# Guessing an attention threshold from part of the keys, and starting two blocks of each step inside the stage in front

## The chip, the cores and the metric

The kernel runs on one core of a Trainium2 chip. The metric is the device time of one execution in microseconds (us), the median of several. A core has TensorE (PE), VectorE (DVE), ScalarE (ACT), GpSimd (POOL) and SyncE (SP, which only issues transfers here); each works through its own list of instructions in order, and they wait for one another by semaphores.

## The reference

Four graph layers over x (4096 nodes, 256 features) with a sparse 4096 x 4096 adjacency. The change touches layer 0 alone, the first of them:

```python
h = relu(layernorm(x))
Xf = Xa = h
for n in range(2):
    q, k = Xa @ W1.T @ W2.T, Xa @ W3.T            # 64 wide
    probs = softmax(q @ k.T)                       # 4096 x 4096
    # keep of each row its largest entries, until their sum reaches 0.9
    A = probs * (sorted_cumsum_before < 0.9);  A = A / A.sum(row)
    Xf, Xa = R @ Xf, A @ Xa                        # R: normalised adj + I
    Z = Z + Xf @ U1[n].T + Xa @ U2[n].T
x = x + layernorm(h + Z)
```

Layers 1 to 3 (a graph convolution, graph attention with four heads, a convolution) follow in the kernel and are not touched.

## The kernel before

**The attention step.** A block is 128 query rows; a step works through 32 of them. For a block, PE makes the logits in four quarters of 1024 keys (`logits`, L1151) into PSUM tiles `pl`, of which there are two; ACT turns each into exponentials of the logit less a guess, with their sum (`exponentials`, L1165). No row is sorted: a threshold is searched. ACT counts and sums what exceeds it (`evaluate`, L1184, a sign pass `s` and a relu pass `r`), twice over 1024 of the keys (`s0 r0`, `s1 r1`) and then over all 4096 (`s2 r2`, `s3`), and after each round DVE works out the next threshold (`aim`, L1196, and `update`, a dozen instructions on 128x1 tiles, ending in `next_pair`, L1265). DVE then lists the largest entries below an upper bound (`below` L1373, `segments` L1381, `listing`), decides the exact threshold, and sets the rest of the row to zero (`cut`, L1433). PE sums over the partitions how many entries tie with the threshold (`ties_pe`, L1456), ACT copies the number (`tied`), and DVE branches on it (`drop`, L1441). Then PE transposes the block in eight tiles (`flip`, L1502), ACT copies each (`take`, L1508), and PE multiplies with the values (`attend`, L1517). In step 0 PE also makes the next step's keys and queries of the block from the result (`next_keys`, L1578 for `kt1`, L1580 for `q`, which is stored to DRAM).

A row whose threshold was not found by its list is counted at the end, and a count other than zero makes the program run `general_layers`, which does all layers again in another way.

**The guess.** What is subtracted in the exponential is the same kind of number for every row: mean and variance of its logits, from the first and second moments of the keys. `by_node` (L969) transposes four 128-column pieces of the keys (eight blocks' worth) and ACT copies them to `kn`; `add_moments` (L975) adds their outer product in PSUM; four rounds cover the 32 blocks. `guess` scales the sums (L982 to L988), multiplies them with 512 queries at a time (L997, L998), sums over the features (L1003), and takes 16 small DVE steps (L1016 to L1030, ending in `minus_guess`), once for the first four blocks and once for the other 28.

**The marks.** In step 0, DVE reduces the adjacency, in 128 pieces of 512 KB, to marks of where it has entries (`marking`, L751), one piece at a time, with four pieces loaded ahead by SP. From the marks, `listed_columns` works out each row's list of columns, by 20 rounds of MAX8 and MATCH_REPLACE8 (L803, L804) and a tail; step 1 gathers rows by these lists on POOL (L844).

**The order.** On DVE, ACT and PE the order is written out by hand (`manual_schedule`), POOL and SP are ordered by the scheduler. `front` is a loop over the 32 blocks with a lag of six (layernorm, relu, transposes L1088, copies L1090, keys and queries L963, L1096, L1097), with a piece of marks at every second turn. Afterwards one table of words per step (`ORDERS`) is walked once per period: a word is an operation, `@k` the offset of the block it is applied to, so a period works on about five blocks at different stages. The place `fill` takes further pieces of guess, marks or lists, by a count per period. `period(b)` runs from -3 to 34. In step 0 `close` runs the last three periods, with the moments of the new keys in the period of b = 32, the rest after it, and the guess for step 1 and `verify` behind the last period.

## Time and profile before

| | us |
|---|---|
| median of three executions | 2958.97 (2954.32 to 2965.91) |
| profiled execution | 2964.31 |
| its span, first to last instruction | 2962.5 |
| PE, DVE, ACT, POOL busy in it | 2470.8, 2349.4, 1989.4, 1216.1 |
| front, to its last copy of queries | 0 to about 96 |
| first exponential of step 0, of step 1 | 113.82, 1125.31 |
| first copy of a transposed attention tile (`at`) of step 0, of step 1 | 220.25, 1223.96 |

The profile is one execution by the hardware's profiler. A row of the waits reads: engine, output tile and line that waited, `<-` what it waited for by engine, tile and line; then the sum, the number and the longest of the waits in us. "DVEq L1441" is DVE's branch. In the table of slices each column is a fortieth of the span. `PEclk` is the clock that TensorE was granted, in tenths. Step 0 runs at a steady 25.5 us a block in its middle, step 1 at about 30.6. The last four blocks of step 0 begin their transposes at 990.5, 1018.06, 1045.48 and 1075.45 us.

### The profile page before, as it was taken

The page shows a single profiled execution, that of the slowest core. Times are in us where ns is not written, and L with a number is a line of the kernel's source. Part 1 is how long each engine was busy: PE and PEld are TensorE (multiplying, and loading weights), DVE is VectorE, ACT ScalarE, POOL GpSimd, SP SyncE. Part 2 cuts the span into 40 slices and gives each one's busy share as a digit, 9 for nine tenths or more (in the row PEclk, how much of TensorE's full clock was granted, in tenths as well). Part 3 has the DMA queues.
Part 4 walks back from the last instruction along what each step waited for, and adds up shares of the span by engine and source line. Part 5 has one row for each costly group of instructions (what it writes and reads, how often), then busy time and mean ns, then how long its engine had stood idle before and what let it go on. Part 6 is the DMA issues. An engine that isn't in the chain of part 4 may idle for free. (4 is left out here: it accounts for less than half of the span.)

```text
span 2962.5 us, 44002 instructions
## 1 busy us (share of the span) xinstructions
PE 2470.8 (83%) x12404; PEld 1867.5 (63%) x12404; DVE 2349.4 (79%) x9531; ACT 1989.4 (67%) x3309; POOL 1216.1 (41%) x1246
## 2 busy tenths in 40 slices
PE   6719999999999985599899889999995766898666
PEld 5407777777777762377667666777773545788444
DVE  5689999999999866888878869999965776898000
ACT  3459999999999724887777768888721226898000
POOL 4100000000000000688888865554534775774676
PEclk8859999999999997799999999999997998999788
DMA  7551222222220012244444443443436764553675
GB/s 236 182 186 52 84 81 72 91 81 72 91 67 26 23 47 84 65 131 125 125 120 133 118 120 114 122 129 106 132 102 215 234 190 140 149 159 92 203 219 160
DMA packets 219611, 361.16 MB, mean 122 GB/s; under 512 B 34519, under 2 KB 151772, under 8 KB 219356
## 3 DMA queue, kind: packets, MB, share of 16 engines
q1 hardware_dynamic: 173708, 237.68, 24.9%
q0 software_dynamic: 44672, 120.34, 14.9%
q8 instruction: 101, 1.65, 0.2%
q14 instruction: 154, 1.26, 0.1%
q10 hardware_dynamic: 976, 0.23, 0.0%
HBM read 290.78 MB, written 67.33 MB: 121 GB/s over the span
## 5 line engine op out<-in xcount | busy, mean ns | idle before, releaser
L1184 ACT ACTIVATE unread<-e,next_pair 128x4096 uint8<-128x4096 f32 (+1 forms) x320 | 859.7, 2686 | 188.2 <-DVE next_pair L1265 145.5
L1517 PE MATMUL pa<-va,at 128*128 128x256 f32 x2048 | 502.7, 391 | 4.7 <-DVE t L1639 4.7
L1517 PE MATMUL pa<-h,at 128*128 128x256 f32 x2048 | 468.6, 379 | 0.1
L1517 PEld LDWEIGHTS pa<-va,at 128*128 128x128 f32 x2048 | 381.9, 196 | 71.8 <-issue 21.2
L1151 PE MATMUL pl<-kt,qb 64*128 64x512 f32 x1024 | 285.9, 666 | 150.4 <-ACT e L1165 150.3
L1517 PEld LDWEIGHTS pa<-h,at 128*128 128x128 f32 x2048 | 376.6, 190 | 44.9 <-ACT at L1508 0.3
L1381 DVE MAX8 best<-near 128x8 f32<-128x256 f32 x1024 | 394.7, 415 | 0.1
L1508 ACT COPY at<-pat 128x512 f32<-128x512 f32 x512 | 284.2, 577 | 161.3 <-PE pat L1502 161.1
L844 POOL DMA_INDIRECT vg<-v_d,column x320 | 305.0, 953 | 122.5 <-issue 92.6
L1502 PE MATMUL pat<-ident,e 128*128 128x128 f32 x2048 | 305.0, 280 | 49.0 <-DVEq L1441 24.3
L1502 PEld LDWEIGHTS pat<-ident,e 128*128 128x128 f32 x2048 | 248.3, 144 | 126.2 <-DVEq L1441 42.5
L859 PE MATMUL acc<-vg,ac 128*128 128x256 f32 x768 | 233.6, 448 | 96.4 <-DMA vg<-v_d,column 71.3
L1165 ACT ACTIVATE e<-pl,minus_guess 128x1024 f32<-128x1024 f32 x256 | 284.0, 1122 | 39.0 <-DVE minus_guess L1030 24.6
L1383 POOL COPY eighth<-best 128x16 f32<-128x16 f32 x64 | 13.2, 205 | 695.6 <-DVE best L1381 695.6
L1373 DVE SCALAR_TENSOR_TENSOR near<-e,end_hi 128x4096 f32<-128x4096 f32 x64 | 286.6, 4478 | 0.1
L1433 DVE SCALAR_TENSOR_TENSOR e<-e,end_t 128x4096 f32<-128x4096 f32 x64 | 286.2, 4472 | 0.0
L844 POOL DMA_INDIRECT vg<-far_d,column x160 | 228.6, 1429 | 129.7 <-DVE e L830 81.3
L859 PEld LDWEIGHTS acc<-vg,ac 128*128 128x128 f32 x768 | 157.0, 221 | 168.2 <-DMA vg<-v_d,column 111.6
L1151 PEld LDWEIGHTS pl<-kt,qb 64*128 64x128 f32 x1024 | 91.3, 196 | 259.9 <-ACT e L1165 223.1
L844 POOL DMA_INDIRECT vg<-mixed_d,column x160 | 205.1, 1282 | 67.7 <-issue 44.1
L2184 PE MATMUL acc<-u,tabg 128*65 128x128 f32 x1536 | 194.2, 281 | 42.7 <-DVE u L2169 41.7
L844 POOL DMA_INDIRECT ac<-in_adjt,adj_row x160 | 199.0, 1244 | 54.3 <-issue 42.2
(557 smaller groups left out, 4306.4 us busy)
## 6 DMA issues: line engine op xcount, KB each, us to landing
adj<-in_adjt SPq DMA_DIRECT2D x128, 512.0 KB
ac<-adjc_d SPq DMA_DIRECT2D x64, 384.0 KB
adjc_d<-ac SPq DMA_DIRECT2D x32, 384.0 KB
ac<-adjc_d SPq DMA_DIRECT2D x32, 320.0 KB
vg<-v_d SPq DMA_DIRECT2D x64, 128.0 KB
targets<-steep_d SPq DMA_DIRECT2D x32, 256.0 KB
vg<-v_d,column POOLq DMA_INDIRECT x320
table_d<-tab SPq DMA_DIRECT2D x32, 132.0 KB
```

Of the source, the lines that this page charges most:

```text
L844: nc.gpsimd.indirect_dma_start(out, None, rows, bass.IndirectOffsetOnAxis(ap=index, axis=0))
L859: nc.tensor.matmul(acc, ac[:, k, :], v[:, k, :], start=(k == 0), stop=(k == CHUNKS))
L1151: nc.tensor.matmul(pl[:, r, :], s["qb"][rows], kt[rows, j * 512 : (j + 1) * 512], start=True, stop=True,)
L1165: nc.scalar.activation(s["e"][:, j * 1024 : (j + 1) * 1024], pl.rearrange("p r c -> p (r c)"), AF.Exp, bias=minus_guess[:, b : b + 1], acc ...
L1184: nc.scalar.activation(unread[:, :width], s["e"][:, :width], func, bias=s["at"], scale=-1.0, accum_out=s["signs"] if func == AF.Sign else ...
L1373: nc.vector.scalar_tensor_tensor(near, s["e"], end["hi"][:, b : b + 1], s["e"], op0=ALU.is_lt, op1=ALU.mult, accum_out=s["low"])
L1381: nc.vector.max(best[:, k, :], near[:, k * (N // SEG) : (k + 1) * (N // SEG)])
L1433: nc.vector.scalar_tensor_tensor(s["e"], s["e"], last, s["e"], op0=ALU.is_ge, op1=ALU.mult, accum_out=s["held"])
L1502: nc.tensor.transpose(pt[:, k, :], s["e"][:, c * P : (c + 1) * P], ident)
L1508: nc.scalar.copy(at, s["pt", g])
L1517: nc.tensor.matmul(s["pa"], s["at", g][:, k, :], va[:, c, :D], start=(c == 0), stop=(c == NB - 1))
L2184: nc.tensor.matmul(s["acc"][:, h, :], s["tab"][:, k, h * (DK + 1) : (h + 1) * (DK + 1)], s["u"][:, k, h, :], start=(k == 0), stop=(k == CH ...
```

## The change

In step 0 the guess takes its moments from the first eight blocks of keys, in step 1 from the first 24 (`SAMPLED`). In step 0 three of the four rounds of moments fall away, and the guess's first part is made inside the front, which also makes three of the four quarters of logits and exponentials of blocks 0 and 1 (`EARLY`); from block 16 on, a block's transposes and keys in the front go to a tile of the ring `pmisc` instead of `pl`. Marks in the front come at two of three turns. Period -3 of step 0 goes, and `fills` are spread over -2 and -1.

In the drain of step 0, the three rounds of moments of step 1 stand in period 30, the guess's first part in period 31, and the first three quarters and the first two search rounds of step 1's block 0 at the end of 31 and in 32; likewise block 1 in 32. The lists' first step stands in 31 and 13 pairs of MAX8 and MATCH_REPLACE8 after it are spread over 32 and 33. What was made early is remembered in `done` and not made again. The early search rounds take their goal from three of the four sums (`aim_part`); the full sum follows with the last quarter. The queries of the first four blocks are read back into one more tile (`first`), and the sums of the moments lie in a `pl` tile together with the guess's. In `listed_columns` the tile for the scratch room is laid out anew, which is left out here, as is `enter`, which hands the tiles of a step to it later. The values `va1` of step 1 are loaded after period -3 instead of -1.

```diff
+SAMPLED = (8, 24)
...
-    def add_moments(r, pm):
+    def add_moments(r, pm, last):
         for k in range(4):
             nc.tensor.matmul(
-                pm[:, : P + 1], kn[:, k, :P], kn[:, k, :], start=(r == 0 and k == 0), stop=(r == 3 and k == 3)
-            )
-    def guess(n, pm):
-        nc.vector.tensor_scalar_mul(mk[:DA, :DA], pm[:DA, :DA], 1.0 / N)
-        nc.vector.tensor_scalar_mul(mk[DA:, :DA], pm[DA:, DA:P], 1.0 / N)
+                pm[:, : P + 1], kn[:, k, :P], kn[:, k, :], start=(r == 0 and k == 0), stop=(r == last and k == 3)
+            )
+    def guess(n, pm, psts, first, nodes):
+        nc.vector.tensor_scalar_mul(mk[:DA, :DA], pm[:DA, :DA], 1.0 / nodes)
+        nc.vector.tensor_scalar_mul(mk[DA:, :DA], pm[DA:, DA:P], 1.0 / nodes)
         both = sm.tile([P, 1], F32, name="both")
-        nc.vector.tensor_scalar_mul(both, pm[:, P : P + 1], 1.0 / N)
+        nc.vector.tensor_scalar_mul(both, pm[:, P : P + 1], 1.0 / nodes)
+        yield
         nc.tensor.matmul(pm[:, 256:257], fold, both, start=True, stop=True)
...
+        mean = l0.tile([P, 1], F32, name=f"mean{n}")
         for lo, hi in ((0, 1), (1, 8)):
-            squares = {}
+            squares, pst = {}, psts(lo)
             for g in range(lo, hi + 1):
...
+                    if g == 0:
+                        yield
+                        nc.vector.tensor_copy(mean, pm[:, 256:257])
...
+                if g == 0:
+                    yield
                 if g > lo:
                     for r in range(4):
...
-                    if lo:
-                        yield
+                    yield
...
-    def front(h0, kt, xs, marked):
+    def front(h0, kt, xs, marked, early):
...
-            if i >= 10 and i % 2 == 0:
+            if i >= 8 and i % 3 != 2:
                 some(marked, 1)
             if 0 <= o + 1 < NB:
                 relu(o + 1)
             if 0 <= o < NB:
-                if o % 2 == 0:
-                    pls[o // 2] = ps.tile([P, 2, 512], F32, name="pl")
-                pt = pls[o // 2][:, o % 2, :256].rearrange("p (k i) -> p k i", k=DC)
+                if o >= 2 * SAMPLED[0]:
+                    pls[o] = ps.tile([P, 512], F32, name="pt", tag="pmisc")
+                elif o % 2 == 0:
+                    both_ = ps.tile([P, 2, 512], F32, name="pl")
+                    pls[o], pls[o + 1] = both_[:, 0], both_[:, 1]
...
-            if 0 <= o - 2 < NB and (o - 2) % 8 == 7:
+            if 0 <= o - 2 < SAMPLED[0] and (o - 2) % 8 == 7:
                 by_node(kt, (o - 2) // 8)
-            if 0 <= o - 3 < NB and (o - 3) % 8 == 7:
-                add_moments((o - 3) // 8, pm)
-        guesses = guess(0, pm)
-        next(guesses)
+            if 0 <= o - 3 < SAMPLED[0] and (o - 3) % 8 == 7:
+                add_moments((o - 3) // 8, pm, SAMPLED[0] // 8 - 1)
+            if o - 4 == SAMPLED[0] - 1:
+                pst = ps1.tile([P, NB, 2], F32, name="pst", tag="pa")
+                guesses = guess(0, pm, lambda lo: pst, near[:, :512], SAMPLED[0] * P)
+            if o - 4 >= SAMPLED[0] - 1:
+                early(o - 3 - SAMPLED[0], guesses)
         return guesses
+    EARLY_GUESSES = (1, 1, 1, 1, 1)
+    EARLY = {
+        6: [(0, "logits0")],
+        7: [(0, "exps0")],
+        9: [(1, "logits0")],
+        10: [(1, "exps0")],
+        14: [(0, "logits2")],
+        15: [(0, "exps2")],
+        17: [(1, "logits2")],
+        18: [(1, "exps2")],
+    }
...
-        def logits(b, half):
+        def logits(b, js):
             s = state[b]
-            if half == 0:
+            if js[0] == 0:
                 s["sums"] = small("sums", 4)
                 s["qb"] = wk.tile([P, P], F32, name="qb")
                 nc.sync.dma_start(s["qb"], q_d[n][:, b * P : (b + 1) * P])
+                s["made"] = set()
             s["pl"] = []
-            for j in (2 * half, 2 * half + 1):
+            for j in js:
+                if j in s["made"]:
+                    continue
+                s["made"].add(j)
                 pl = ps.tile([P, 2, 512], F32, name="pl")
...
+        def aim_part(b):
+            goal, skip = small("part_goal"), small("skip", 4)
+            state[b]["part_goal"] = goal
+            nc.vector.scalar_tensor_tensor(
+                skip[:, :3],
+                state[b]["sums"][:, :3],
+                (1.0 - TOP_P) / 3.0,
+                fours[:, :3],
+                op0=ALU.mult,
+                op1=ALU.mult,
+                accum_out=goal,
+            )
+            yield
         def measured(b, k):
             s = state[b]
-            width, goal = (PART, end["goal"][:, b : b + 1]) if k < 2 else (N, s["full_goal"])
+            width, goal = (PART, s.get("part_goal", end["goal"][:, b : b + 1])) if k < 2 else (N, s["full_goal"])
...
+                if "part_goal" in s:
+                    yield from aim(b)
...
-            calls[f"logits{h}"] = of_block(logits, h)
+            calls[f"logits{h}"] = of_block(logits, (2 * h, 2 * h + 1))
             calls[f"exps{h}"] = of_block(exponentials)
+        calls["logits2"], calls["exps2"] = of_block(logits, (2,)), of_block(exponentials)
...
+        done = set()
+        def early(b, *names):
+            for name in names:
+                if name in calls:
+                    done.add((name, b))
+                    calls[name](b)
+                else:
+                    steps, _, *k = chains[name]
+                    for _ in line(steps, b, *k) if k else chain(aim_part(b), update(b, 0)):
+                        pass
+                    lines[(steps, b, *(k or (None,)))] = iter(lengths[steps] * [None])
+        def period(b, fills=(), pieces=((),) * 4, inserts={}):
             pieces = iter(pieces)
@@ -1869,41 +1934,17 @@
                     for fill, k in zip(fills, next(pieces)):
                         some(fill, k)
                 elif name in calls:
-                    calls[name](b + int(off))
+                    if (name, b + int(off)) not in done:
+                        calls[name](b + int(off))
                 else:
                     woven(name)(b + int(off))
-                if name in ("take1", "take3", "take5") and b + int(off) == NB - 1:
-                    some(between, 2)
-        def moments(pm):
-            for r in range(3):
-                by_node(kt1, r)
-                yield
-                add_moments(r, pm)
-                yield
-        def close(lists):
-            for g in range(4):
-                cols = slice(g * 1024, min((g + 1) * 1024, (NB - 2) * P))
-                nc.sync.dma_start(near[:, cols], q_d[1][:, cols])
-            some(lists, 1)
-            pm = ps.tile([P, 2, 512], F32, name="pl").rearrange("p r c -> p (r c)")
-            period(NB, between=moments(pm))
-            period(NB + 1)
-            some(lists, 10)
-            for b in range(NB - 2, NB):
-                nc.scalar.copy(near[:, b * P : (b + 1) * P], state[b]["q"])
-            by_node(kt1, 3)
-            add_moments(3, pm)
-            period(NB + 2)
-            guesses = guess(1, pm)
-            next(guesses)
-            verify()
-            return guesses
-        return period, verify, close
+                for insert in inserts.get(name, ()):
+                    insert()
+        def query(b):
+            return state[b]["q"]
...
+        period, verify, enter, early, query = layer0_step(0, kt0)
+        period1, verify1, enter1, early1, _ = layer0_step(1, kt1)
+        def ahead(i, guesses):
+            some(guesses, EARLY_GUESSES[i] if i < len(EARLY_GUESSES) else 0)
+            for b, words in EARLY.get(i, ()):
+                early(b, *words.split())
         with tc.tile_pool(name="front", bufs=1) as xs, tc.manual_schedule(engines=MANUAL):
-            guesses = front(h0, kt0, xs, marked)
+            guesses = front(h0, kt0, xs, marked, ahead)
         own = st.enter_context(tc.tile_pool(name="own0", bufs=1))
         with tc.manual_schedule(engines=MANUAL):
-            period, verify, close = layer0_step(0, h0, kt0, own, marked)
-            early = {
-                -3: ((0, 2), (0, 2), (3, 2), (0, 2)),
-                -2: ((3, 4), (9, 4), (9, 4), (9, 4)),
-                -1: ((0, 3), (0, 3), (0, 3), (0, 3)),
-            }
-            for b in range(-3, NB):
-                period(b, (guesses, marked), early.get(b, ((0, 0),) * 4))
+            enter(h0, own, marked)
+            fills = {-2: ((2, 3), (2, 3), (2, 3), (2, 3)), -1: ((0, 4), (0, 4), (0, 4), (0, 4))}
+            for b in range(-2, NB - 2):
+                period(b, (guesses, marked), fills.get(b, ((0, 0),) * 4))
             some(marked, NB * QUARTERS)
+            pm = ps.tile([P, 2, 512], F32, name="pl")
+            first = adj_pool.tile([P, CA, P], F32, name="adj").rearrange("p l i -> p (l i)")[:, :512]
+            nc.sync.dma_start(first, q_d[1][:, :512])
             lists = listed_columns(marks, e_pool.tile([P, N], F32, name="e"), ps)
-            guesses = close(lists)
+            def sums_of(lo):
+                if lo:
+                    return ps1.tile([P, NB, 2], F32, name="pst", tag="pa")
+                return pm[:, 1, : 2 * NB].rearrange("p (b k) -> p b k", k=2)
+            guesses = guess(1, pm[:, 0], sums_of, first, SAMPLED[1] * P)
...
+            def ahead1(b, words):
+                return lambda: early1(b, *words.split())
...
+            period(
+                NB - 2,
+                inserts={
+                    "take1": [nodes(0)],
+                    "take2": [sums(0)],
+                    "take3": [nodes(1)],
+                    "take4": [sums(1)],
+                    "take5": [nodes(2)],
+                    "take6": [sums(2)],
+                    "take7": [guessing(1)],
+                },
+            )
+            period(
+                NB - 1,
+                inserts={
+                    "take1": [guessing(1)],
+                    "attend1": [guessing(1)],
+                    "take3": [guessing(1), listing(1)],
+                    "flip4": [guessing(1)],
+                    "attend7": [ahead1(0, "logits0")],
+                    "turn": [ahead1(0, "exps0 logits2 exps2 s0 r0")],
+                },
+            )
+            queries()
+            period(
+                NB,
+                inserts={
+                    "cut": [ahead1(0, "u0")],
+                    "ties": [ahead1(0, "s1 r1")],
+                    "drop": [listing(1), ahead1(0, "u1")],
+                    "take1": [listing(1), ahead1(1, "logits0")],
+                    "take2": [listing(2), ahead1(1, "exps0 logits2 exps2 s0 r0")],
+                    "take3": [listing(1), ahead1(1, "u0 s1 r1")],
+                    "take4": [listing(1), ahead1(1, "u1")],
+                    "take5": [listing(2)],
+                    "take6": [listing(1)],
+                    "take7": [listing(1)],
+                    "turn": [listing(1)],
+                },
+            )
+            period(
+                NB + 1,
+                inserts={
+                    "keys": [last_queries, ahead1(0, "logits1 exps1")],
+                    "xa_pe": [listing(2)],
+                    "copy_xa": [ahead1(0, "s2 r2")],
+                    "h_pe": [verify],
+                },
+            )
+            period(NB + 2)
     with ExitStack() as st:
         s1 = st.enter_context(tc.tile_pool(name="s1", bufs=1))
         vg_pool = st.enter_context(tc.tile_pool(name="vg1", bufs=3))
         va1 = s1.tile([P, NB, D], F32, name="va1")
         with tc.manual_schedule(engines=MANUAL):
-            period, verify, close = layer0_step(1, va1, kt1, s1, vg_pool)
+            enter1(va1, s1, vg_pool)
             fill = by_turns(guesses, lists)
-            pieces = {-3: (0, 3, 2, 3), -2: (2, 3, 2, 2), -1: (2, 2, 99, 0)}
+            pieces = {-3: (3, 3, 2, 3), -2: (2, 3, 2, 2), -1: (2, 2, 99, 0)}
             for b in range(-3, NB + 4):
-                period(b, (fill,), [(k,) for k in pieces.get(b, (0, 0, 0, 0))])
-                if b == -1:
+                period1(b, (fill,), [(k,) for k in pieces.get(b, (0, 0, 0, 0))])
+                if b == -3:
                     for q in range(8):
                         bs = slice(q * NB // 8, (q + 1) * NB // 8)
                         nc.sync.dma_start(va1[:, bs, :], blocks(heads_d)[:, bs, :])
-            verify()
+            verify1()
```

## The prediction

> **What bounds the kernel now.** The order of views was: the page's table of forty slices, then the busy time by stretch, the waits inside the two poor stretches, and the single instructions where the long waits end.
>
> A slice of the span is 74 us; digits are tenths busy.
>
> ```profile
> PE   6719999999999985599899889999995766898666
> ...
> DVE  5689999999999866888878869999965776898000
> ACT  3459999999999724887777768888721226898000
> ...
> PEclk8859999999999997799999999999997998999788
> DMA  7551222222220012244444443443436764553675
> ```
>
> Slices 4 to 13 are step 0 of the attention at its steady pace: all three engines at 9, no DMA limit. Work is lost at the front (slices 1 to 3) and where step 0 drains into step 1 (14 to 16). The change touches nothing of the steady stretches, so its worth is in those two. By stretch (PE, PEld, DVE, ACT, POOL busy us and instructions, granted clock, DMA share, GB/s):
>
> ```profile
> 97.00:220.00 123.00, 44.88 (x164) 22.07 (x163) 93.82 (x297) 66.14 (x78) 0.38 (x2) 0.65 0.53 178
> ...
> 1118.00:1222.00 104.00, 45.43 (x144) 20.62 (x144) 80.99 (x327) 63.85 (x74) 23.35 (x18) 0.63 0.24 71
> ```
>
> The first runs from the end of the front to the first transposed attention tile of step 0, the second likewise for step 1. PE has 45 us of work in each; DVE is nearest to full (76% and 78%). The reader sees a latency chain of DVE and ACT, not a throughput limit. The waits, for 85 to 220, 1000 to 1120 and 1120 to 1240 us:
>
> ```profile
> ACT unread L1184 <- DVE next_pair L1265: 29.2, 4, 16.8
> ACT e L1165 <- DVE minus_guess L1030: 16.6, 1, 16.6
> DVE marks L751 <- DMA adj<-in_adjt: 7.0, 9, 1.8
> ```
>
> ```profile
> DVE mk L982 <- PE pl L975: 16.3, 1, 16.3
> ...
> PE pat L1502 <- DVEq L1441: 7.5, 3, 4.2
> ```
>
> ```profile
> ACT unread L1184 <- DVE next_pair L1265: 20.9, 5, 8.1
> ACT unread L1184 <- DVE steep L1249: 8.5, 3, 4.5
> ...
> ACT e L1165 <- DVE minus_guess L1030: 8.0, 1, 8.0
> ```
>
> ACT cannot start a step's first exponential before DVE has the guess (16.6 and 8.0 us), and then waits for each new threshold behind DVE's marks. Where ACT restarts (start, us, instruction, idle before):
>
> ```profile
> 113.82 1.11 ACT L1165 ACTIVATE e<-pl,minus_guess 128x1024 f32<-128x1024 f32 x1 [16.56 <-DVE minus_guess L1030]
> 161.42 3.71 ACT L1184 ACTIVATE unread<-e,next_pair 128x4096 uint8<-128x4096 f32 x1 [16.84 <-DVE next_pair L1265]
> 194.52 3.71 ACT L1184 ACTIVATE unread<-e,next_pair 128x4096 uint8<-128x4096 f32 x1 [8.84 <-DVE next_pair L1265]
> ```
>
> ```profile
> 1125.31 1.11 ACT L1165 ACTIVATE e<-pl,minus_guess 128x1024 f32<-128x1024 f32 x1 [8.04 <-DVE minus_guess L1030]
> ```
>
> **The change, first place: the front.** Three of four rounds of by_node and add_moments go: 3 x (1.06 + 1.06) = 6.4 us of PE and 3 x 0.58 of ACT. Six quarters of logits come in, four PE records each. Sixteen records took 6.2 us at 115, so 1.56 us a quarter; two took 1.12 us at 97, so 2.24. Six are 9.4 to 13.4 us, and PE gets 3 to 7 us more. Six exponentials of 1.1 us fall on ACT, busy 31.6 of 97 us. DVE gets six more marks of 1.2 us and the guess's first part (two 0.7 us passes, sixteen small ones of 0.19): 8 to 12 us, against 42 idle us of which 31.8 are waits for PE's keys. In the second half a block's pt tile moves from the logits' buffers to the other ring of two, so its transposes wait for the copy two blocks back; the copies already set the pace there (0.4 to 0.5 us a block), so I add nothing. If that ring stalls, it costs up to 0.4 us x 16. Front end: 95.6 to 99, +3.5, ends 0 and +10.
>
> A rule speaks against new PE work here. The Trainium skill (TensorE: Matmul & The Clock Gate, "What's actually happening") says that the array's clock is halved after an idle window of about 3.4 us and is freed only by as much sustained work. A quarter would then be 3.1 us, six 18.7, the front's end about +9 and the whole sum -37 instead of -42. The trace grants 0.84 to 0.86 in the front's middle and 1.0 in its last 17 us, and its slowest quarter there is 2.24; I go by the row, 1.6 to 2.2, and keep the rule for the upper end.
>
> **From the front to the first attend of step 0.** Before, guess and marks hold DVE from 98.95 to 113.8, then four exponentials reach 120.0, where s0 stands. After, blocks 0 and 1 have three quarters ready, one quarter is left: logits 1.6, exp 1.1, so s0 at about 101.4 (-18.6). r2 of block 0 ends at about 117 (136.2 before). Period -3 and eight marks (9.7 us of DVE) leave this stretch; 28 remain, of 36. The s3 of block 0 came 25 us after that, with marks in between; with three or four fewer it comes at about 138 (161.4). The s3 of block 1, 58 us after r2 before, at about 173 (194.5), since there the last 17 marks run into DMA: 0.5 MB each lands in 1.6 to 1.75 us at the 300 to 328 GB/s seen, against 1.2 us of DVE. The two qb loads no longer stand in SP's queue between adj loads (they stopped it 113 to 125 and 164 to 173), so adj is fed without a break. First attend 199.5 against 219.6: -20. Bounds: -8 if the DVE chain between s0 and attend keeps its 100 us and only the guess's 14.9 minus the front's growth is saved; -26 if adj never limits. I take -20, near the DVE sum: 93.8 - 9.7 - 6 = 78 us of work in 100.
>
> **Second place: the drain.** Three rounds of moments (2.1 us PE each, kn copy 0.58) move from the period of block 31's attention to the one two earlier, which is full: +5 us. The next period gets the guess's first part from the sums of 24 blocks and the lists' first step (L986, L997, L1003, L778: 3.5 us of PE) and three logits quarters of step 1's block 0 (4.7): +7 to 8 us on PE. On ACT three exponentials, s0 and r0 (5.7 us) stand ahead of tied for block 31; behind tied wait the branch L1441 and all flips of that block. Against it: the cut of block 31 (1070.77) no longer stands behind the lists' first step, which waited 8.3 us for pt. The flips of block 31 so start at about 1090.5 instead of 1075.45: +15. In the last period -7 of moments and -2.2 of logits leave, three quarters of block 1 (4.6) and about 3 us of stalls come: even. kt of block 31 is copied at about 1125 instead of 1110.06. Bounds for the drain: +5 (PE's 4.2 us wait and ACT, 41 busy of 118, hide the rest) and +30 (everything inserted is serial). Cover of the moved lists (11 pairs of 2.58 us): DVE's idle 16.3 us at 1101.7 to 1118 and the periods' other gaps; without it, +12.
>
> **The restart of step 1.** Before, from kt at 1110.06: guess to 1125.3, four exponentials, three rounds of search, r2 of block 0 done at 1156.3 (+46). After, the guess and two rounds are behind it: keys, logits 1.6, exp 1.1, s2 and r2 3.7 each: done 10 us after kt, 1135, -21. Then DVE's leftovers (7 list pairs 18.1, seven L998 passes of 0.75, found's checks 3.2, small ones) fill 30 us before the update: s3 of block 0 about 1155 (1165). Block 1 has three quarters and two rounds too: its r2 ends at 1166 (1187.9). From there as before; the first attend 1200 against 1222.6: -22, ends -8 and -32. The lists' gathers start at about 1166 (1193 before), so POOL isn't late. qb and first loads are small (64 and 256 KB) in a stretch where DMA is at 0.2 to 0.3: nothing.
>
> **Sum.** -20 - 22 = -42 us: the steps after keep their lengths and shift whole. The profiled execution took 2964.3 us with a span of 2962.5; the median shown is 5.3 below it. 2959 - 42 = 2917. With the bounds -26 - 32 and -8 - 8: 2901 to 2943.
>
> **Rivals.** (1) Half of it: the front saves its 20 but the restart is held by DVE's leftovers (80% of DVE used there) and step 1's gathers, or the other way round: about -20, 2939. For it: the 8.5 us waits on steep show DVE to be the chain of the restart; against it, its work total falls. (2) The drain is serial: +30 instead of +15 makes the second place -7; with the lists' +12 uncovered it is +5, and with the front at its poor end, -8, the sum is -3: 2956, no change. For it: PE is at 104 of 118 us in the drain and its queue is in order; against it: the waits of 4.2 and 16.3 us are room. (3) Slower: the guess from 1024 of 4096 keys (3072 in step 1) is too far off, and a row's threshold falls outside its list. Then found isn't all ones, the last check sends the program into general_layers, which does every layer again: above the 2110 us that the attention takes here, over 5000 in all. One row of 8192 decides it; the guess only sets the scale and the start of a search that goes on for the same number of rounds with the true sums, and in the arithmetic of the kernel's formulas on the given inputs the fullest list holds 28 of 32 and 38 of 40: very unlikely.
>
> **How the numbers follow.** Forecast 0.66, rival 1 0.19, rival 2 0.11, rival 3 0.04. The time is the forecast's, 2917, with its own range 2901 to 2934. 2896 to 2949 takes in the half gain and the better ends and leaves 2 in 10 out, mostly above. 0.5% is 14.8 us, about what a measurement of this kernel tells from none. Faster by more: the forecast and most of rival 1, 0.82; within: the rest of it and most of rival 2, 0.12; slower 0.06.
>
> **What would show it.** ACT's first exponentials before 80 us in the front; s0 of block 0 about 101; s3 at 138; first at copy of step 0 near 200 and of step 1 some 42 us earlier than 1224, near 1182. Periods of step 0 unchanged at 25.5 us. The 16.6 and 8.0 us waits for minus_guess gone, the flips of block 31 15 us later relative to their start of the steady stretch. Wrong if the front ends after 105, if next_pair waits above 30 us remain before the first attend, or if PE waits on ACT's e at several quarters in the drain.

## The result, and the profile after

The changed kernel takes 2944.7 us (median of six, 2943.4 to 2947.1) against 2961.6 for the kernel before beside it (2954.3 to 2965.9): a ratio of 0.9944, interval 0.9931 to 0.9958, 17 us less. Forecast were 42 us less. The profiled execution fell from 2964.3 to 2943.4 us, 21 less, and its trace is laid beside the one of before. The table of slices of the changed kernel:

```profile
PE   5729999999999986798988989999995776898666
...
DVE  5789999999999879888878879999965776898000
ACT  2469999999999835887867878788621226898000
...
PEclk8769999999999987899999999999997998999788
DMA  6651222222220013244444434333437765553675
```

The two weak places are still there: slices 1 to 3 are hardly fuller, while 15 to 17 are (8, 6 and 7 for PE where 8, 5 and 5 stood; the forecast called them 14 to 16). Two stretches say it more sharply, from the front's end to step 0's first attention tile, and the restart of step 1 (columns as before: PE, PEld, DVE, ACT, POOL, clock, DMA share, GB/s):

```profile
106.00:214.00 108.00, 40.30 (x126) 21.99 (x124) 84.62 (x278) 59.27 (x66) 0.38 (x2) 0.60 0.53 176
1116.00:1192.00 76.00, 38.70 (x128) 20.64 (x127) 69.88 (x262) 49.28 (x53) 27.97 (x25) 0.64 0.39 115
```

From the last queries of the front to step 0's first attention copy it was 124.6 us and is 107.8. From the copy of block 31's keys to step 1's first attention copy it was 113.9 us and is 76.1, with DVE busy for 92% of the stretch shown. ACT restarts here in the changed kernel:

```profile
106.81 1.11 ACT L1197 ACTIVATE e<-pl,minus_guess 128x1024 f32<-128x1024 f32 x1 [2.94 <-PE pl L1183]
...
107.92 1.14 ACT L1216 ACTIVATE unread<-e,ones 128x1024 uint8<-128x1024 f32 x1
```
```profile
147.55 3.71 ACT L1216 ACTIVATE unread<-e,next_pair 128x4096 uint8<-128x4096 f32 x1 [4.14 <-DVE next_pair L1312]
```
```profile
187.99 3.71 ACT L1216 ACTIVATE unread<-e,next_pair 128x4096 uint8<-128x4096 f32 x1 [15.91 <-DVE next_pair L1312]
```

The wait for the guess is gone, but the chain starts at 107.9 instead of the 101.4 forecast, and the 15.9 us before the last pass over block 1 (`s3`, forecast at 173, found at 188.0) are a wait that should have shrunk.

How far the changed kernel is ahead of the one before, by the same instruction in both traces (us; minus is earlier):

| | forecast | found |
|---|---|---|
| last queries copied in the front (95.7 before) | +3.5 | +10.3 |
| first attention copy of step 0 (220.3) | -20 | -6.5 |
| the same of block 28 (991.8) | -20 | -5.8 |
| the same of block 31 (1076.3) | -5 | +9.4 |
| first attention copy of step 1 (1224.0) | -42 | -30.0 |
| block 16 of step 1 (1723.5) | -42 | -26.4 |
| block 21 of step 1 (1886.3) | -42 | -26.8 |
| block 24 of step 1 (1979.8) | -42 | -20.6 |
| end of the span (2962.5) | -42 | -20.9 |

The blocks of step 0 keep their length: 27.7 us in the middle in both traces, not the 25.5 given above. A front does not take the same time in every execution. In three traces with the front of before (its own and those of two runs below), step 0's first attention copy came at 220.3, 222.7 and 226.4 us, in four with the changed front at 212.1 to 214.3: the gain there is 6.5 us in this pair and 9.8 between the means.

So there are three questions: why the front and the start of step 0 gave 6.5 instead of 20; whether the drain did what it seems to have done; and what took 9 us back inside step 1.

### The profile page after: what moved, and what is told of

Same layout as the page of the kernel before. It is cut to its first block, busy times and chain, and to the rows that moved or that the text cites. A ratio compares the mean times of both kernels' runs of the same rounds, so it can differ in the third digit from the quotient of the medians.

```text
span 2941.6 us, 43924 instructions
## 1 busy us (share of the span) xinstructions
PE 2463.4 (84%) x12356; PEld 1864.1 (63%) x12356; DVE 2351.0 (80%) x9538; ACT 1986.3 (68%) x3305; POOL 1221.3 (42%) x1246
## 5 line engine op out<-in xcount | busy, mean ns | idle before, releaser
L1183 PE MATMUL pl<-kt,qb 64*128 64x512 f32 x1024 | 278.1, 653 | 115.2 <-ACT e L1197 112.1
L846 POOL DMA_INDIRECT ac<-in_adjt,adj_row x160 | 235.2, 1470 | 56.0 <-issue 41.1
L846 POOL DMA_INDIRECT vg<-mixed_d,column x160 | 205.0, 1281 | 67.0 <-issue 44.4
L846 POOL DMA_INDIRECT vg<-far_d,column x160 | 191.7, 1198 | 85.9 <-issue 48.5
```

The lines of the kernel that those rows point to most:

```text
L846: nc.gpsimd.indirect_dma_start(out, None, rows, bass.IndirectOffsetOnAxis(ap=index, axis=0))
L1183: nc.tensor.matmul(pl[:, r, :], s["qb"][rows], kt[rows, j * 512 : (j + 1) * 512], start=True, stop=True,)
```

## The experiments

The first four runs were made on another chip, where step 1's first half ran at 43 us a block instead of 31 and the kernel before took 3261 us; they are compared with it there, and with each other.

**The front: when the first marks come.** DVE early in the front, before and then changed, with the instruction of ACT that waited in the changed one:

```profile
18.98 0.27 DVE L1054 SCALAR_TENSOR_TENSOR x<-x,x 128x4 f32<-128x4 f32 x1
...
25.14 1.22 DVE L751 TENSOR_REDUCE marks<-adj 128x8 f32<-128x1024 f32 x1 [2.54 <-DMA adj<-in_adjt]
```
```profile
25.80 1.22 DVE L754 TENSOR_REDUCE marks<-adj 128x8 f32<-128x1024 f32 x1 [6.57 <-DMA adj<-in_adjt]
26.93 0.15 DVE L1059 SCALAR_TENSOR_TENSOR x<-x,x 128x4 f32<-128x4 f32 x1
```
```profile
27.12 0.60 ACT L1062 ACTIVATE h<-e,x,x 128x256 f32<-128x256 f32 x1 [10.83 <-DVE x L1059]
```

The first mark now comes one loop turn sooner, ahead of the shift (L1059; L1054 before) that ACT's next four relus need. Its piece of the adjacency lands no sooner than before: the kernel before waited 2.5 us for it, but behind that shift, which it had made at 19.0. The next run makes the first mark at turn 15 of the loop instead of 9. The keys of block 2 came 8.7 us late, and 7.4 were still missing at block 9.

```diff
-            if i >= 8 and i % 3 != 2:
+            if i >= 15 and (i % 3 != 2 or i < 27):
                 some(marked, 1)
```

> The changed kernel with the same 22 marks in the front, but the first one five loop turns later, so that it no longer stands ahead of the third group's shift and relu while its adjacency piece is still in flight. Theory (the front's 10 us are one wait of 6.6 us for the first adjacency piece and what it starts): the front ends near 97.5 instead of 105.9, the first attention copy of step 0 comes near 205 instead of 213.7, and the time falls by about 8 us to 2936. Rival (the front is long because of the logits and marks put into it): the front still ends at 103 or later and the time stays within 3 us of 2944.7.

Measured: 3229.2 us, ratio 0.9899 (0.9878 to 0.9921). Block 2's queries were ready at 23.0 instead of 29.7 us (the run of the front alone, below, has the front of the changed kernel on the same chip), and block 9's at 44.4 instead of 50.4: the wait was what the theory says. But blocks 10 to 31 then took 64.7 us instead of 57.1, and the front ended at 109.1, not 97.5. The first attention copy came at 216.5 against 214.3. So the wait is real, and something took more than its worth back. Two things differ there: the marks stand closer together, one at each of twelve turns, and TensorE's granted clock was 0.84 from 44 to 109 us, against 0.91 from 50 to 107 in the front alone. Which of the two cost the 7.6 us is not shown.

**The start of step 0: marks ahead of a goal.**

```diff
-            fills = {-2: ((2, 3), (2, 3), (2, 3), (2, 3)), -1: ((0, 4), (0, 4), (0, 4), (0, 4))}
+            fills = {-2: ((2, 3), (2, 3), (2, 3), (2, 3)), -1: ((0, 2), (0, 2), (0, 2), (0, 2))}
```

> The changed kernel with two marks instead of four at each fill of period -1, eight fewer ahead of block 2's first goal; the marks' words of the later periods make up for them. Theory (after the front DVE is the limit, and marks stand ahead of the thresholds): the wait of 15.9 us for a threshold before the second pass over block 1 shrinks by 8 to 10 us, the first attention copy of step 0 comes near 205, the time near 2936. Rival (the adjacency loads or the search's own latency set it): the copy stays within 2 us of 213.7.

Measured: 3223.6 us, ratio 0.9881 (0.986 to 0.9901). The first attention copy came at 199.8 instead of 214.3, 14.6 us for eight marks of 1.2 us, since the DMA waits that stood before some of them went too (5.4 us in the front alone, 1.3 here). The restart in question, in this run:

```profile
174.03 3.71 ACT L1216 ACTIVATE unread<-e,next_pair 128x4096 uint8<-128x4096 f32 x1 [0.81 <-DVE next_pair L1312]
```

15.9 us of waiting have become 0.8. The marks put off come back in later periods, where most cost nothing: 1.9 of the 14.6 us are lost again by block 28, in two periods that had no marks and now have three each (28.0 and 27.8 us instead of 27.1 and 26.8).

**The two halves.** In one run the drain is that of before, in the other the front is; the core of each edit:

```diff
-            for b in range(-2, NB - 2):
+            for b in range(-2, NB):
                 period(b, (guesses, marked), fills.get(b, ((0, 0),) * 4))
...
+            period(NB, inserts={k: [lambda: some(two, 2)] for k in ("take1", "take3", "take5")})
+            period(NB + 1)
+            some(lists, 10)
...
+            guesses = guess(1, pm, sums_of, near[:, :512], N)
+            some(guesses, 5)
+            verify()
```

(Here `two` makes three rounds of moments.)

> Only the front's half of the change; the drain of step 0 and the restart of step 1 are those of the kernel before. Theory (the two halves add, and a shift of step 0 passes to the end whole): step 1's first attention copy 6.5 us earlier than before, the time 6 us below before, ratio 0.998. Rival (the front's gain is lost later, in step 1): no difference from before.

```diff
-SAMPLED = (8, 24)
+SAMPLED = (32, 24)
...
-            if i >= 8 and i % 3 != 2:
+            if i >= 10 and i % 2 == 0:
...
+    EARLY_GUESSES = (5,)
+    EARLY = {}
...
+            for b in range(-3, NB - 2):
```

> Only the drain's half of the change; front and first periods of step 0 are those of the kernel before. Theory (the restart gives 24 us at step 1's first attention copy and step 1 takes some 9 back, since its first half is paced by GpSimd's gathers): 1200 us for that copy, the end about 15 us earlier than before, ratio 0.995. Rival (what step 1 took back was an accident of one profile): the end 24 us earlier, 0.992.

Measured: the front alone 3260.7, ratio 0.9995 (0.9982 to 1.0008); the drain alone 3235.9, ratio 0.9909 (0.9883 to 0.9935). By these times the drain carries the whole gain. The traces say where the front's half went. It was 12.1 us ahead of the run with the old front at step 0's first attention copy (214.3 to 226.4) and still 11.5 at block 28; step 0 keeps a lead. Inside step 1, between blocks 21 and 23, it fell behind that run by a further 5.8 us, at the place that block 22 below is about. The 15 us expected of the drain alone became 25: the drain alone does not lose those 6 us, and the rest of the difference is not explained (step 1's first half runs otherwise on this chip).

**Step 1: do the gathers take the lead back?** Between blocks 0 and 16 of step 1 the lead fell from 30.0 to 26.4 us. POOL is busy there for 400 of 505 us, nearly all of it with gathers. The next two runs replace 160 of the 320 gathers of that half.

```diff
-                for i in range(CHUNKS):
-                    gather(ac[:, i, :], adj_rows, adj_row[:, i, d : d + 1])
+                nc.sync.dma_start(ac[:, :CHUNKS, :], adjt[d, :, :CHUNKS, :])
```

The changed kernel itself was run again beside them.

> The changed kernel itself beside the experiments of this call. Theory and rival agree: ratio 0.994 if the chip is like the first; on a chip where step 1's first half is slowed by its gathers the ratio may differ, since more or less of the lead is taken back there.

> The changed kernel, but step 1 fetches the adjacency rows of its first half not by five gathers a block on GpSimd but by one plain load of the same size from the same array; the rows are other ones, so layer 0's mixed values and all that follows are not the reference's. 160 of 640 gathers go. Theory (the gathers of step 1's first half set its pace, 320 of them at 1.65 us each): its periods fall from 31 to about 28 us, 40 us less in all, and the lead of step 1's first attention copy over the kernel without these gathers (next run) is still whole at step 1's end. Rival (the engines' own work sets the pace): under 10 us less.

> The kernel before with the same replacement of the row gathers by plain loads, which again leaves out the right rows. Theory: 40 us less than the kernel before, and 24 to 30 us more than the changed kernel with the same replacement, instead of the 17 between the two whole kernels. Rival: the distance between the two stays 17.

Measured: changed 2944.2 (ratio 0.9936, 0.9914 to 0.9958); without the row gathers 2913.0 for the changed kernel and 2934.9 for the one before. The gathers do pace that half, though by 31 and 28 us, not 40. Without them the lead is 31.6 us at the first attention copy and 31.6 at block 16, where it had fallen by 3.6 with them. It then goes to 29.2 by block 21, where the two whole kernels stood at 26.8. So the gathers account for some 2 to 4 us of what was lost. But the distance of these two kernels is 21.9, not 24 to 30, and the drop between blocks 21 and 24 is there as before (29.2 to 23.2). It had another cause.

**Step 1: block 22.** In the trace of the changed kernel, on DVE behind the cut of that block:

```profile
1884.72 4.48 DVE L1482 SCALAR_TENSOR_TENSOR e<-e,end_t 128x4096 f32<-128x4096 f32 x1
...
1889.72 0.28 DVE L1492 TENSOR_SCALAR drop<-eights,end_extra,end_t 128x8 f32<-128x8 f32 x1
...
1890.12 4.41 DVE L1495 MATCH_REPLACE8 e<-drop,e 128x4096 f32<-128x4096 f32 x1
```

`drop` works only where an entry ties with its row's threshold. The trace of before has no instruction of it; this one has one block with it, and so have the front alone and the two runs with other marks, while the drain alone has none. The guess is subtracted in the exponent, so another guess rounds all entries of step 0, and with them step 1's rows, otherwise. The front alone has the changed guess in step 0 only, the drain alone in step 1 only: the tied block came with step 0's guess, and it takes back some 6 us of what the front's half gives. The next experiment starts from a kernel that takes both findings on the marks together:

```diff
-            if i >= 8 and i % 3 != 2:
+            if i >= 12 and i % 3 != 2:
...
+            fills = {-2: ((2, 4), (2, 4), (2, 4), (2, 4)), -1: ((0, 2), (0, 2), (0, 2), (0, 2))}
```

> The changed kernel with the first mark of the front three turns later (20 marks there, not 22, no denser than before), four instead of three at each fill of period -2 and two instead of four in period -1. Theory (the first mark's wait for its piece costs the front 6 us, and marks ahead of block 2's goal 14 us): the front ends near 100, the first attention copy of step 0 near 195, and the ratio is about 0.008 below that of the changed kernel beside it. Rival (the marks put off come back as a block of work at the end of the marks or the front is slow for its own sake): the ratio stays within 0.003 of it.

Measured: 2928.7, ratio 0.9884 (0.9857 to 0.9911), 15.5 us below the changed kernel beside it where 24 were expected. The front ended at 101.9 (104.3 beside it), the first attention copy of step 0 came at 198.4 (212.1); 195 was expected. This and the three later runs that keep this front show what the first mark's place was worth: they end it at 98.9 to 101.9 us, 100.3 in the mean, where four traces of the changed front have a mean of 105.5 and three of the old one 97.0. With another constant on top:

```diff
-            nc.vector.scalar_tensor_tensor(v, y, -1.2816, v, op0=ALU.mult, op1=ALU.add)
+            nc.vector.scalar_tensor_tensor(v, y, -1.28, v, op0=ALU.mult, op1=ALU.add)
```

> The kernel with later and fewer marks, and in both guesses the factor -1.2816 replaced by -1.28; every row's threshold search starts from slightly other numbers, so that all exponentials are rounded otherwise, and no instruction is added or moved. Theory (in step 1's block 22 one row's entry ties with its threshold only in the rounding that the new guess brings, and the branch then runs a pass of 4.4 us over the block): with other rounding no tied block appears in the trace, step 1's periods are even there, and the time is 6 us below that of the kernel with later and fewer marks. Rival (the 6 us there come from the order or from transfers): the period of block 22 is long again.

Measured: 2922.2, ratio 0.9845 (0.9828 to 0.9861). No instruction of `drop` is in its trace, and its lead over before is 40.8 us at block 21 and 40.9 at block 24, where that of later and fewer marks falls from 38.8 to 32.6. The 6.2 us were the tied block. The order of the work is the same in both runs: that one guess meets a tie and another does not is chance.

**The drain: ScalarE ahead of the tie count.**

```diff
-                    "turn": [ahead1(0, "exps0 logits2 exps2 s0 r0")],
...
-                    "cut": [ahead1(0, "u0")],
-                    "ties": [ahead1(0, "s1 r1")],
-                    "drop": [listing(1), ahead1(0, "u1")],
-                    "take1": [listing(1), ahead1(1, "logits0")],
...
+                    "ties": [ahead1(0, "exps0")],
+                    "drop": [listing(1)],
+                    "take1": [listing(1), ahead1(0, "logits2 exps2 s0 r0")],
+                    "take2": [listing(1), ahead1(0, "u0 s1 r1")],
+                    "take3": [listing(2), ahead1(1, "logits0"), ahead1(0, "u1")],
...
```

> The kernel with later and fewer marks, but in the drain the first exponentials and search passes of step 1's block 0 stand behind the last block's keys and its copy of the tie count on ScalarE, and are spread over the takes. Theory (5.7 us of ScalarE ahead of that copy hold up the last block's branch and transposes): block 31's first attention copy comes 5 to 6 us earlier, step 1's first attention copy about 4 us earlier, and the time is some 4 us below that of later and fewer marks. Rival (the restart is paced by VectorE's lists and checks): block 31 earlier, step 1's first copy unchanged.

Measured: 2922.4, ratio 0.9851 (0.9834 to 0.9867). Both traces on ACT, later and fewer marks first:

```profile
1062.35 0.59 ACT L1587 COPY zt<-pt 128x512 f32<-128x512 f32 x1 [3.79 <-PE pt L1582]
1062.83 1.12 ACT L1197 ACTIVATE e<-pl,minus_guess 128x1024 f32<-128x1024 f32 x1
...
1068.79 0.57 ACT L1607 COPY hu<-pu 128x512 f32<-128x512 f32 x1
...
1072.09 0.14 ACT L1511 CAST tied<-pkq 1x1 int32<-1x1 f32 x1
```

```profile
1057.56 0.59 ACT L1587 COPY zt<-pt 128x512 f32<-128x512 f32 x1 [3.79 <-PE pt L1582]
1058.04 0.59 ACT L1607 COPY hu<-pu 128x512 f32<-128x512 f32 x1
...
1060.45 0.14 ACT L1511 CAST tied<-pkq 1x1 int32<-1x1 f32 x1
```

From `zt` to `tied` 9.7 us became 2.9. Block 31's first copy came 11.9 us earlier, 8.6 of them from the drain (this run was 3.3 us ahead already at step 0's first copy, the front's doing). Step 1's first copy came at 1175.1 instead of 1183.5: 8.4 us earlier, 5.1 more than it brought along, and at step 1's last block 8.4 were left. So the theory held, in the drain and at the restart, and the rival did not. The run with both edits, below, says the same beside the one with the other constant alone: 8.1 us of its own at block 31, 4.8 at step 1's first copy, 4.9 at its last block. Some 3.5 of the 8.6 us do not arrive. DVE is busy for 66.3 of the 73 us from 1102 to 1175 there, so it has little room at the restart; that this is what keeps the 3.5 back is argued, not shown. The 2922.4 and the 2928.7 were measured on two chips, and the intervals of the two ratios overlap.

**The front: what the early quarters cost.**

```diff
-    EARLY = {
-        6: [(0, "logits0")],
-        7: [(0, "exps0")],
...
-    }
+    EARLY = {24: [(0, "logits0 exps0")]}
```

> The changed kernel without the early quarters of the front: only the first half of block 0 is made, after the last keys; block 1 wholly later. Guess and marks in the front stay. Theory (the front's second half is not longer for the six quarters): the front still ends within 1.5 us of 105, and the first attention copy of step 0 comes 4 to 8 us later. Rival (the six quarters lengthen the front by 7 us or more): it ends near 98.

Measured: 2963.4 in its single timed execution, 2967.4 for before. With less to do the front ended 14.3 us later, at 120.3, not at 98 or 105. Both theories were wrong. The same edit again, and a run with products in the places of the quarters that nothing reads:

```diff
+            for j in {6: (0, 1), 9: (0, 1), 14: (2,), 17: (2,)}.get(i, ()):
+                pl = ps.tile([P, 2, 512], F32, name="pl")
+                for r in range(2):
+                    rows = slice(r * DA, (r + 1) * DA)
+                    nc.tensor.matmul(pl[:, r, :], ident[rows], kt0[rows, j * 512 : (j + 1) * 512], start=True, stop=True)
```

> The kernel without early logits once more. Theory (its slow front is TensorE at half clock, because no stretch of the second half keeps TensorE busy long enough): granted clock near 0.5 from 80 us to the front's end, which comes near 119 again. Rival (an accident of one execution): clock above 0.8 and the front's end near 104.

> The kernel without early logits, and at the places where the changed kernel makes the six quarters, as many products of the same shape into the same buffers, which nothing reads. Theory (the products lift the clock, and the clock sets the front's pace): granted clock near 1.0 from 80 us on and the front's end at 102 to 106, though TensorE has more to do. Rival (the pace has another cause): the front's end near 119 as without them, or later.

Measured: 2959.2 and 2951.5 (2962.9 for before). The stretch from 80 to 104 us of the changed kernel, of the repeat, and of the unread products (PE busy and instructions first, clock third from the end):

```profile
80.00:104.00 24.00, 18.01 (x125) 13.49 (x122) 17.02 (x41) 12.85 (x28) 10.85 (x14) 1.00 0.72 225
```
```profile
80.00:104.00 24.00, 17.67 (x76) 15.54 (x76) 13.04 (x36) 6.59 (x16) 9.37 (x12) 0.50 0.54 179
```
```profile
80.00:104.00 24.00, 17.90 (x114) 13.14 (x111) 15.66 (x40) 8.19 (x19) 11.04 (x15) 0.93 0.69 214
```

The front ended at 120.7 in the repeat and at 107.7 with the unread products. TensorE is busy 18 of 24 us in all three; at half clock it gets 76 instructions done, at full clock 114 to 125. Four key products took 1.06 us in the slow front and 0.61 in the fast one. Products that nothing reads give the front 13.0 us back, and with them the clock: it is the clock that sets the pace here, not the work that the quarters add. The kernel before, with its rounds of moments in that half, was granted 0.86 from 60 to 80 us and 1.00 from 80 to 97.

**Together.** The run with the tie count first, with the other constant:

> Later and fewer marks, the tie count's copy first, and the other guess constant, together. Theory (the three causes are independent): no tied block, the time 6 us below that of the kernel with the tie count's copy first, 2916, ratio 0.983. Rival: the ratio stays at 0.985.

Measured: 2918.5 us (2918.1 to 2918.8), ratio 0.9849 (0.983 to 0.9868), 25.7 us under the changed kernel's 2944.2. No tied block in the trace, and the lead of 46 us is the same at blocks 16 and 31 of step 1 (46.4 and 46.2). Beside the run without the other constant (2922.4, on another chip) that is 4 us, and the ratio stays at 0.985, as the rival has it; the intervals overlap. The 6 us are seen in the traces alone: from block 21 to 24 the run without the other constant takes 100.2 us, this one 93.4.

## Why the prediction was wrong

Of the 42 us forecast, 13.5 are missing at step 0's first attention copy and 9 were lost inside step 1; the restart gave 2 more than forecast.

*The front, +3.5 forecast, +10.3 found, outside its bounds by a little.* The forecast's own sign of being wrong, a front that ends after 105, was there (105.9). The step that failed counted DVE's added work against its idle time. The idle time was there, but the first added instruction stood in front of a needed one and waited 6.6 us for a transfer that could not be earlier. With that mark behind the shift, and two marks fewer in the front, the front was 3.3 us longer than the old one between the means, about the +3.5. The logits, weighed at 9 to 13 us, cost no time, and a quarter took 1.0 to 1.1 us of PE. Their price was misread: the two records of 1.12 us at 97 are a whole quarter (in the changed kernel four records take the same 1.13), and the 1.56 of 115 was measured at a clock of 0.50 to 0.76, so doubling it to 3.1 halved the clock twice. The rule of the Trainium skill on the clock (TensorE: Matmul & The Clock Gate, "What's actually happening") was put forward as speaking against the added products, at 3.1 us each. The traces show its other side, that work frees the clock: with the products it was 0.93 to 1.00 from 80 to 104 us, without them 0.50, and the front is then 14 us longer.

*From the front to the first attention, 100.5 us forecast, 107.8 found.* The sum of DVE's work was about right (84.6 us found, 78 forecast); that the chain would shrink with it was not. 28 marks were counted by their total and not by where they stand: the 16 of period -1 stood ahead of the threshold that block 1's last pass waits for, and eight fewer gave 14.6 us.

*The drain and the restart, +15 and -37 forecast, +15.1 and -39.4 found.* Right in size, and the moved work did leave the restart. `tied_first` shows the ScalarE term: ACT's inserted work delays block 31 by 8.6 us, and 5.1 of them reach step 1's first copy. That DVE's leftovers set the pace of the rest, as the forecast's step for s3 had it, fits its 92% there and was not tested.

*"The steps after keep their lengths and shift whole."* Held in step 0 and failed in step 1 by 9 us: 6.2 for a tied block that the other rounding brings, and about 3 in the half that the gathers pace, which rival 1 named. The forecast said that the search goes on for the same number of rounds, and overlooked `drop`, a branch that depends on the data. That this guess met a tie was bad luck; that the branch can be met at all was a term put at nothing.

Rival 1 (half of it, 2939, chance 0.19) was nearest: a gain of about 20 us, found as 21 in the profiled execution and 17 in the medians. Of its two ways, "or the other way round" is the one that came: the restart gave its share and the front did not. But a third of the loss was the tied block, which it does not have, so that its number is so near is partly luck.

## What to carry to other kernels

Work put into an engine's idle time must be asked what its first instruction waits for and who stands behind it; a total of idle microseconds does not answer that. Count inserted work between a goal and the instruction that feeds it, not over the stage. Compare the lead at several instructions along both traces: here it showed in one table that the half that looked easy had failed, that the hard one had worked, and that a data-dependent branch took 6 us back. One pair of traces is thin ground for a few microseconds: the same front differed by 6 us from one execution to another.

## What the hardware showed that was not expected

A TensorE that is 77% busy can stay at half clock. With gaps of 0.7 to 0.9 us between its groups of matmuls it had 0.50 for some 40 us, in two executions of two; the repeat:

```profile
78.00:120.00 42.00, 32.48 (x140) 29.08 (x140) 21.06 (x54) 10.79 (x25) 13.02 (x17) 0.50 0.57 180
```

Six quarters of added products, 6.5 us of useful or 7.8 of unread ones, raised it to 1.00 or 0.93, and the unread ones shortened the front by 13 us. The skill's section on the clock has it freed after about 3.4 us of sustained work and halved after an idle window as long. The first agrees with the slow front, where a group lasts 2.4 us. The second does not cover the unread products, where the clock fell at 90.3 us (0.50 from 92 to 93.5) though no gap since 74 us was above 1.0:

```profile
88.06 0.61 PE L965 MATMUL pt<-vt,w 128*128 128x128 f32 x4
...
90.10 0.41 PE L1096 MATMUL pt<-ident,h 128*128 128x128 f32 x2 [0.98 <-DVE near L1105]
90.35 1.02 PE L965 MATMUL pt<-vt,w 128*128 128x128 f32 x4
```

Gathers on POOL mostly take 0.95 us, but 33 of the 320 in step 1's first half took over 2 us, 4.7 on average, in the changed kernel's trace.
